# Two-layer vision block on one core: one group's last mixed channels loaded apart and measured two chunks on, steps without pieces spread in one group, constant products at first

## The chip, the cores and the metric

The kernel runs on one core of a Trainium2 chip. The metric is the device time of one execution in microseconds (us), as the median of several runs. A core has a matrix engine (TensorE, in the profile PE for products and PEld for weight loads), VectorE (DVE), ScalarE (ACT), GpSimd (POOL), and SyncE (SP), which here issues every DMA in the order written. The engines run apart from each other and each takes its own instructions in order.

## The reference

The input `x` is (2, 56, 56, 384) in float32: two images of 3136 tokens with 384 channels. Two layers follow each other.

```
# layer 0
h = neighborhood_attention(layer_norm(x), w_qkv, b_qkv, rpb, w_proj, b_proj, heads=12, k=7)
x = x + h
x = x + gelu(layer_norm(x) @ w1 + b1) @ w2 + b2          # 384 -> 1536 -> 384
# layer 1
p = layernorm(x) @ w_in + b_in                            # 384 -> 768
local = depthwise 3x3 convolution of p
mixed = 0.25 * (four running means of local: left, right, up, down) + local
x = x + layernorm(mixed) @ w_out + b_out                  # 768 -> 384
x = x + gelu(layernorm(x) @ w1 + b1) @ w2 + b2
```

In the attention, each token attends to the 7 x 7 tokens around it (moved inward at the borders), with a bias per head and offset. The running means are first-order filters (decay 0.6, gain 0.4) along rows and columns, in both directions.

## The kernel before

**Attention.** The tokens are cut into 14 groups `n` of 448 (8 rows of one image), and each group into 4 windows of 8 x 14 tokens. One window and one of three sets of four heads (`hg`) make a step `s`, so that a group has 12 steps, `k = s % 12`. In step `s` TensorE makes the scores of the step (L515, tile `sc`, two PSUM banks), where two steps with two chunks of keys each share one go; VectorE adds the bias (L530, `pts`), ScalarE takes the exponential, VectorE adds the chunks up (L546, `sum`), and TensorE multiplies the numerators of step `s - 2` with the values (L556, `o`) and adds them up (L563, `sums`). After a window's last set, VectorE turns the sums (L482), GpSimd copies them (L484, `totals`), VectorE inverts them (L488) and watches their size (L492, `good`), GpSimd widens them (L494, `wide`), VectorE turns and multiplies (L498, L500).

Beside the step stands at most one *piece* for later groups, taken from the list `ahead`: a query or key block (L386, six passes of 448 columns) or a tile of values (L424, six passes of 384). At k = 0 the list is filled with 9 or 10 pieces; `spare` names the steps without one, which are (3, 4, 5) where there are 9, and else (4, 6). Up to group 10 a projection of an earlier group (L582) can stand beside the step too. Group 11 has 9 pieces and no projections.

`load_residual(t)` loads a tile of the input for the sum after the projection and sets a count of steps (4 in the first use), after which `add_bias` lets GpSimd add a row to it (L576). The first three tiles are loaded ahead of the step loop, all with the same count.

**Before the step loop.** The first group is normalized, turned by TensorE (L357) and put through the key, value and query products. PSUM tiles come from `any_bank`, four banks in turn. `ident` (128 x 128 unit matrix) and `ones_hd` (128 x 32, all ones) are constants made on chip.

**Layer 0's MLP and layer 1** work on groups of up to 512 tokens. In the last part, `dgroups` are the groups of layer 1's MLP: four tiles of 128 tokens each, the last two groups smaller. `half_way` is the first of them which reaches into the second image; here it is group 6, with 64 tokens of image 0 and 448 of image 1. The convolution and the running means run as jobs of `beside`, an object that puts VectorE work between the products by estimated cost: first `Band` jobs (rows), then per image six `Columns` jobs, one for each 128 of the 768 channels. The job `(1, 5)` is the last one. A `Columns` job ends with two stores of its half images to `mix_d` (L1259). `beside.until(name)` puts out all steps up to the end of a job at once.

`load_mix(g)` loads a group's mixed values, all six channel blocks, to the tile `mx` (L1274). For `half_way` it does so in pieces of 128 tokens, after `beside.until((1, 5))`; it is called behind the last output tile of group 4. While group 5's hidden layer runs, 12 chunks `m` of 6 passes (L1080), `measure_beside` makes the statistics of group 6: `measure` turns one tile of 128 tokens by TensorE (L1288, `xi`) and VectorE takes mean and variance (L214, L215). For `g <= half_way` this is done behind chunks m = 3, 5, 7, 9, and `close`, which makes the inverse deviation (L219 on VectorE, L222 on GpSimd), behind m = 10. Groups after `half_way` are measured on VectorE alone. Behind m = 11 `project_out` multiplies `mx` with `w_out`.

Of the kernel before, what the change touches and what calls it, by code (L numbers as in the profile page):

```python
# [41 lines left out]
NH, KS, HD = 12, 7, 32  # L42
P = 128
NC = C // P
INNER, NI = 2 * C, 2 * C // P
HID, NHID = 4 * C, 4 * C // P
# [127 lines left out]
def block_kernel(ctx: ExitStack, tc: tile.TileContext, ins: dict, out: bass.AP):  # L174
    nc = tc.nc
# [11 lines left out]
    mix_d = [dram.tile([NI, P, H * W], F32, name=f"mix_d{b}") for b in range(B)]  # L187

    ident = const.tile([P, P], F32, name="ident")
# [101 lines left out]
    ones_hd = lp.tile([P, HD], F32, name="ones_hd")  # L291
# [87 lines left out]
    def any_bank():  # L379

        return ps_s.tile([P, GT], F32, name="ps", tag="any")
# [186 lines left out]
    def load_residual(t, pool=lp, bufs=3, steps=4):  # L568

        xrs[t] = pool.tile([P, C], F32, name="xr", bufs=bufs)  # L570
        nc.sync.dma_start(out=xrs[t], in_=xf[t * P : (t + 1) * P, :])
        loaded[t] = steps
# [33 lines left out]
    def load_group(src, group, tag):  # L606
        t0, n = group
        t = xp.tile([P, NT, C], F32, name=tag)
        nc.sync.dma_start(
            out=t[:, :n, :], in_=src[t0 : t0 + n * P, :].rearrange("(k p) c -> p k c", p=P)  # L610
        )
        return t
# [29 lines left out]
            nc.sync.dma_start(out=dst, in_=src)  # L642


    tps = [any_bank() for c in range(NC)]
    halves = [Norm(sm) for h in range(2)]
    for h, norm in enumerate(halves):
# [39 lines left out]
        channels_of(2, c, any_bank)()  # L687
    load_bias(0, 3)
    for t in range(3):
        load_residual(t)  # L690
    shift_by_values(ep, ps_t, wproj, shift)
    sctx.close()

# [13 lines left out]
    for s in range(NU + 4):  # L707
        n, k, hg, i = s // UG, s % UG, s % NC, s // NC
        if s == NU:

            kctx.close()
            xp = ctx.enter_context(tc.tile_pool(name="x", bufs=2, side="right", reuse_waits="tile"))
            tail_pool = actx.enter_context(tc.tile_pool(name="a_tail", bufs=1))
            xs = {g: load_group(x1f, groups[g], "xa") for g in range(2)}
            for t in range(T2 // P - 4, T2 // P):
                load_residual(t, tail_pool, 4, 2)
        store_all()
        while load:
            load_residual(load.pop(0))
        if k == 0 and n < ng:  # L720
            vals = []
            if n + 1 < ng:
                ahead += [lambda n=n, m=m: query_or_key(n + 1, m, one_bank) for m in range(NC)]
                vals += tiles_of(n + 1)[2:]
            if n + 2 < ng:
                vals += tiles_of(n + 2)[:2]
            ahead += [lambda t=t: value(t, one_bank) for t in vals]
            if n + 2 < ng:
                ahead += [
                    lambda n=n, m=m: query_or_key(n + 2, m, one_bank) for m in range(NC, 2 * NC)  # L730
                ]

            spare = (3, 4, 5) if len(ahead) == 9 else (4, 6)

        if k == 2 and n + 4 < ng:
            load_x(n + 4)
        if k == 1 and n < ng:
            load_bias(n, NWC - 1)
        if n + 1 < ng and k in (4, 10):
            load_bias(n + 1, 0 if k == 4 else 1)  # L740
        if s == NU - UG - 4:
            ectx.close()
            wm = ctx.enter_context(tc.tile_pool(name="w_mlp", bufs=1, side="right"))
            w1, w2, w_parts = weights(0)
        if s < NU and hg == 2 and s + 1 < NU:
            ws[i + 1] = Window(i + 1)
        if s >= NU - UG - 4 and hg == 2 and w_parts:
            w_parts.pop(0)()

        if s <= NU:  # L750
            for take in taking:
                take()
            taking = []
        if s == NU + 1:
            sctx.close()
            ps_s = sctx.enter_context(tc.tile_pool(name="a_pss", bufs=4, space=PSUM))
        if s < NU:

            if s not in units:
                units[s] = Unit(ws[i], hg)  # L760
                units[s].scores()
                behind = Unit(ws[(s + 1) // NC], (s + 1) % NC) if s + 1 < NU else None
                if behind is not None and (units[s].m + behind.m) * TT <= BANK:
                    behind.scores(units[s].m)
                    units[s + 1] = behind
        new, before, last = units.get(s), units.get(s - 1), units.pop(s - 2, None)
        done = last.w if last is not None and last.hg == NC - 1 else None
        if last is not None:
            last.values()
        behind = ws.get(i - 1 - (hg == 0))  # L770
        if behind is not None and hg == 2:
            behind.invert()
        if behind is not None and hg == 0:
            behind.divide()
            if behind.j == NWC - 1:
                to_project += tiles_of(behind.n)
            ws.pop(behind.i)
        if n + 3 < ng and k < NT:
            measure_x(n + 3, k)
        for half in range(2):  # L780
            if new is not None:
                new.biased(half)
                new.numerators(half)
            if half == 0 and done is not None:
                done.take()
        if before is not None:
            before.gathered()
        if done is not None:
            done.gather()
        if n < END:  # L790
            if ahead and k not in spare:
                taking.append(ahead.pop(0)())
            if to_project and n < END - 1:
                taking.append(project(to_project.pop(0), turning_bank))
        elif ahead:
            if k != 3:
                taking.append(ahead.pop(0)())
        elif s - END * UG in THEN:
            taking.append(project(to_project.pop(0), one_bank))
        elif s > NU and s < NU + 4 and to_project:  # L800
            taking.append(project(to_project.pop(0), any_bank))
        for t in list(loaded):
            loaded[t] -= 1
            if loaded[t] < 0:
                add_bias(t)
        if n + 3 < ng:
            if k in (4, 5):
                for q in range(2 * k - 8, 2 * k - 6):
                    normalize_x(n + 3, q)
            if k in (8, 9, 11):  # L810
                taking.append(channels_of(n + 3, (8, 9, 11).index(k), turning_bank))
# [159 lines left out]
    def passes(xs, xn, w1, w2, between=lambda ps: None):  # L971
# [12 lines left out]
        beside = Beside()  # L984

        def images(t, n):


            for b in range(B):
                lo, hi = max(t, b * T1), min(t + n, (b + 1) * T1)  # L990
                if lo < hi:
                    yield b, lo - b * T1, lo - t, hi - lo
# [273 lines left out]
        def load_mix(g):  # L1266
            t0, n = dgroups[g]
            mx = io.tile([P, NI, MT], F32, name="mx")

            step = P if g == half_way else n * P  # L1270
            for t in range(0, n * P, step):
                for b, at, here, size in images(t0 + t, step):
                    here += t
                    nc.sync.dma_start(  # L1274
                        out=mx[:, :, here : here + size],
                        in_=mix_d[b][:, :, at : at + size].rearrange("m p t -> p m t"),
                    )
            x = load_group(x2_d, dgroups[g], "xa")
            if g >= half_way:
                add_row(x, dgroups[g][1], "b_out")  # L1280
            return mx, x, Norm(sm)

        def measure(mx, norm, k):
            parts = []
            for h in range(2):
                ps = ps_t.tile([P, NC, P], F32, name="xi", tag="pt")
                for c in range(NC):
                    nc.tensor.transpose(  # L1288
                        ps[:, c, :], mx[:, h * NC + c, k * P : (k + 1) * P], ident
                    )  # L1290
                parts.append(ps.rearrange("p c q -> p (c q)"))
            norm.add(k, parts)
# [12 lines left out]
        def measure_beside(m, g, ahead):  # L1305


            n = dgroups[g][1]
            if g > half_way:
                if m % 2 == 0 and m // 2 < n:  # L1310
                    measure_by_vector(ahead[0], ahead[2], m // 2)
            elif m % 2 == 1 and 0 < m // 2 <= n:
                measure(ahead[0], ahead[2], m // 2 - 1)
            if m == 10:
                ahead[2].close(n)

        def project_out(g, mx, x, inner):
# [174 lines left out]
        for g, (t0, n) in enumerate(dgroups):  # L1492
# [37 lines left out]
                    add_row(x3, dgroups[g + 1][1], "b2_1")  # L1530
                beside.go(ROW_D)
            if g + 2 == half_way:
                beside.until((1, NI - 1))
                ahead = load_mix(g + 2)
        pctx.close()

# [90 lines left out]
```

## Time and profile before

| | us |
|---|---|
| median of 3 runs (lowest, highest) | 2680.19 (2678.64, 2681.08) |
| the profiled execution's own time | 2680.04 |
| its span, first to last instruction | 2678.2 |
| TensorE products of the hidden layers (L1080), busy | 771.1 |
| VectorE busy, all | 1963.2 |
| TensorE clock granted, mean | 0.996 |

The span is what the trace covers; the difference of 1.84 us to the execution's own time lies around it. In 40 slices of about 67 us the page gives the busy tenths of the products and the granted clock:

```profile
PE   8999999999899999999999999999999899999999
...
PEclk9999999999999999999999999999999999999999
```

A 9 means 90% or more, so that only the first slice, the eleventh and the thirty-second show idle time here, and a few microseconds at a lower clock do not show at all. In lists of instructions below, a line has the start, the duration, the engine, the line of the kernel, the operation, what it writes and reads, the tile sizes and types and how many were merged, and in brackets the idle time just before it with what ended it.

### The profile page before, as it was taken

The page shows a single profiled execution, that of the slowest core. Times are in us where ns is not written, and L with a number is a line of the kernel's source. Part 1 is how long each engine was busy: PE and PEld are TensorE (multiplying, and loading weights), DVE is VectorE, ACT ScalarE, POOL GpSimd, SP SyncE. Part 2 cuts the span into 40 slices and gives each one's busy share as a digit, 9 for nine tenths or more (in the row PEclk, how much of TensorE's full clock was granted, in tenths as well). Part 3 has the DMA queues.
Part 4 walks back from the last instruction along what each step waited for, and adds up shares of the span by engine and source line. Part 5 has one row for each costly group of instructions (what it writes and reads, how often), then busy time and mean ns, then how long its engine had stood idle before and what let it go on. Part 6 is the DMA issues. An engine that isn't in the chain of part 4 may idle for free. (4 is left out here: it accounts for less than half of the span.)

```text
span 2678.2 us, 37275 instructions
## 1 busy us (share of the span) xinstructions
PE 2640.3 (99%) x14963; PEld 1473.9 (55%) x14963; DVE 1963.2 (73%) x3539; ACT 898.7 (34%) x1447; POOL 249.7 (9%) x264
## 2 busy tenths in 40 slices
PE   8999999999899999999999999999999899999999
PEld 4666666656655455555555555555555455555556
DVE  3778877876365698688989889888988627677652
ACT  4555555554322332223344422311143211111111
POOL 1111111111211100000010000000010011101100
PEclk9999999999999999999999999999999999999999
DMA  6323454224411132233346544533346401111000
GB/s 216 134 89 102 154 170 146 80 77 158 156 37 38 65 107 88 89 128 105 123 156 230 184 149 150 178 120 114 118 182 228 152 19 37 45 44 39 30 12 17
DMA packets 134249, 298.99 MB, mean 112 GB/s; under 512 B 11463, under 2 KB 89905, under 8 KB 131761
## 3 DMA queue, kind: packets, MB, share of 16 engines
q1 hardware_dynamic: 134064, 296.50, 32.3%
q8 instruction: 119, 1.95, 0.3%
q14 instruction: 66, 0.53, 0.1%
HBM read 180.86 MB, written 115.61 MB: 111 GB/s over the span
## 5 line engine op out<-in xcount | busy, mean ns | idle before, releaser
L1080 PE MATMUL mm<-hT,w 128*128 128x512 f32 (+2 forms) x1872 | 771.1, 569 | 0.4 <-ACT hT L254 0.2
L1080 PEld LDWEIGHTS mm<-hT,w 128*128 128x128 f32 x1872 | 352.7, 190 | 383.5 <-issue 352.1
L1089 ACT ACTIVATE hid<-mm,chan 128x512 f32<-128x512 f32 (+2 forms) x312 | 206.1, 661 | 683.3 <-PE mm L1080 683.2
L1096 PE MATMUL y_end<-w,hid 128*128 128x384 f32 x1200 | 395.2, 486 | 0.0
L1174 DVE SCALAR_TENSOR_TENSOR loc<-pt,taps,loc 128x990 f32<-128x990 f32 (+9 forms) x336 | 377.1, 1122 | 10.0 <-ACT loc L1156 1.7
L1096 PE MATMUL y<-w,hid 128*128 128x384 f32 x1152 | 379.4, 486 | 0.0
L1096 PEld LDWEIGHTS y_end<-w,hid 128*128 128x128 f32 x1200 | 227.5, 190 | 157.2
L1096 PEld LDWEIGHTS y<-w,hid 128*128 128x128 f32 x1152 | 218.2, 190 | 150.5 <-issue 1.0
L530 DVE TENSOR_TENSOR pts<-sc,bias 119x448 f32<-119x448 f32 (+3 forms) x336 | 220.9, 699 | 78.2 <-PE sc L515 75.2
L536 ACT ACTIVATE pts<-pts 119x448 f32<-119x448 f32 (+3 forms) x336 | 206.8, 642 | 191.3 <-DVE pts L530 187.9
L222 POOL TENSOR_TENSOR rs<-rs,mhalf 128x4 f32<-128x4 f32 (+4 forms) x67 | 87.1, 1300 | 1727.0 <-DVE rs L219 1691.6
L386 PE MATMUL ps<-hT,wqkv 128*128 128x448 f32 x504 | 212.0, 559 | 2.0 <-ACT qT L396 0.7
L1064 DVE STREAM_TRANSPOSE hT<-xn 32x96 f32<-32x96 f32 x672 | 181.1, 269 | 31.4 <-PE mm L1080 11.8
L1080 PE MATMUL mm<-hT,w_in 128*128 128x512 f32 (+2 forms) x468 | 191.9, 568 | 0.6 <-ACT hT L254 0.6
L240 ACT ACTIVATE xn<-xc,sh,rs 128x384 f32<-128x384 f32 x98 | 64.7, 698 | 268.6 <-DVE sh L233 268.5
L1080 PEld LDWEIGHTS mm<-hT,w_in 128*128 128x128 f32 x468 | 88.5, 190 | 102.1 <-issue 90.6
L386 PEld LDWEIGHTS ps<-hT,wqkv 128*128 128x128 f32 x504 | 90.2, 191 | 82.8 <-issue 73.1
L515 PEld LDWEIGHTS sc<-qT,kT 32*100 32x100 f32 (+3 forms) x3168 | 91.6, 170 | 67.1 <-issue 17.9
L1299 DVE STREAM_TRANSPOSE turned<-mx 32x192 f32<-32x192 f32 x336 | 123.3, 367 | 4.2
L515 PE MATMUL sc<-qT,kT 32*100 32x112 f32 (+3 forms) x3168 | 114.7, 272 | 6.5 <-DVE pts L530 5.8
L556 PE MATMUL o<-pts,vt 100*32 100x112 f32 (+3 forms) x3168 | 112.7, 266 | 3.8 <-DMA vt<-v_d 2.7
L582 PE MATMUL ps<-wproj,og 128*128 128x384 f32 x294 | 107.1, 503 | 3.6 <-DVE xr L590 3.6
(104 smaller groups left out, 2644.9 us busy)
## 6 DMA issues: line engine op xcount, KB each, us to landing
bias<-in_bias_t SPq DMA_DIRECT2D x16, 1344.0 KB
loc<-loc_d SPq DMA_DIRECT2D x24, 784.0 KB
mixed<-mix_d SPq DMA_DIRECT2D x24, 784.0 KB
mix_d<-mixed SPq DMA_DIRECT2D x24, 784.0 KB
xa<-x_d SPq DMA_DIRECT2D x22, 768.0 KB
p_d<-mx SPq DMA_DIRECT2D x10, 1536.0 KB
mx<-mix_d SPq DMA_DIRECT2D x10, 1536.0 KB
pt<-p_d SPq DMA_DIRECT2D x18, 560.0 KB
```

The source lines that it names most:

```text
L386: nc.tensor.matmul(ps, lhsT=wqkv[:, c, m * P : (m + 1) * P], rhs=hT[:, c, half_of(n)], start=c == 0, stop=c == NC - 1,)
L515: nc.tensor.matmul(sc[i // 2][: w.keys, i % 2, (first + c) * TT : (first + c + 1) * TT], lhsT=kT[d, hg, w.keys_at + r * w.kc : w.keys_at + ...
L530: nc.vector.tensor_tensor(self.of(half), sc[half][:n, :, at].rearrange("p h (c q) -> p h c q", q=TT), self.w.bias[:n, 4 * self.hg + h : 4 ...
L536: nc.scalar.activation(self.of(half), self.of(half), AF.Exp)
L556: nc.tensor.matmul(o[i * HD : (i + 1) * HD, hg, :], lhsT=w.vt[:n, c, h * HD : (h + 1) * HD], rhs=self.pts[:n, i, c, :], start=c == 0, stop ...
L582: nc.tensor.matmul(ps, lhsT=ogs[t // 7][:, c, at : at + P], rhs=wproj[:, c, :], start=c == 0, stop=c == NC - 1,)
L1064: nc.vector.transpose(hT[j : j + HD, :, k * P + i : k * P + i + HD], xn[i : i + HD, k, :].rearrange("p (c q) -> p c q", c=NC)[:, :, j : j ...
L1080: nc.tensor.matmul(ps[:, : n * P], lhsT=w[:, c, m * P : (m + 1) * P], rhs=hT[:, c, : n * P], start=c == 0, stop=c == NC - 1,)
L1089: nc.scalar.activation(t[:, : n * P], ps[:, : n * P], AF.Gelu, bias=col(b1, m))
L1096: nc.tensor.matmul(ps, lhsT=t[:, k * P : (k + 1) * P], rhs=w[:, m, :], start=m == 0, stop=m == len(lhs) - 1,)
L1174: nc.vector.scalar_tensor_tensor(to, pt[:, lo + dy - self.top : hi + dy - self.top, xt : xt + n], self.tap(dy, dx), to, ALU.mult, ALU.add,)
L1299: nc.vector.transpose(t[j : j + HD].rearrange("p (m c) -> p m c", m=NI)[:, :, i : i + HD], mx[i : i + HD, :, k * P + j : k * P + j + HD],)
```

## The change

There are four edits. Before the first group's work, twelve products of `ones_hd` and `ident` are written to a bank that nothing reads. The first three residual tiles get a count of 8 steps in place of 4. In group 11 (`END - 1`) the steps without a piece are k = 3, 6, 9. For `half_way`, the mixed values are loaded in two parts: channel blocks 0 to 4 after the job (1, 4), block 5 after the job (1, 5), each for all tokens of the group in one DMA per image; its tiles are measured behind m = 5, 7, 9, 11 and the statistics closed behind m = 11.

```
+    warm = any_bank()
+    for _ in range(12):
+        nc.tensor.matmul(warm[:HD, :P], lhsT=ones_hd, rhs=ident, start=True, stop=True)
     tps = [any_bank() for c in range(NC)]
...
     for t in range(3):
-        load_residual(t)
+        load_residual(t, steps=8)
...
             spare = (3, 4, 5) if len(ahead) == 9 else (4, 6)
+            if n == END - 1:
+                spare = (3, 6, 9)
...
             mx = io.tile([P, NI, MT], F32, name="mx")
-            step = P if g == half_way else n * P
-            for t in range(0, n * P, step):
-                for b, at, here, size in images(t0 + t, step):
-                    here += t
+            def load_channels(lo, hi):
+                for b, at, here, size in images(t0, n * P):
                     nc.sync.dma_start(
-                        out=mx[:, :, here : here + size],
-                        in_=mix_d[b][:, :, at : at + size].rearrange("m p t -> p m t"),
+                        out=mx[:, lo:hi, here : here + size],
+                        in_=mix_d[b][lo:hi, :, at : at + size].rearrange("m p t -> p m t"),
                     )
+            if g == half_way:
+                beside.until((1, NI - 2))
+                load_channels(0, NI - 1)
+                beside.until((1, NI - 1))
+                load_channels(NI - 1, NI)
+            else:
+                load_channels(0, NI)
...
                     measure_by_vector(ahead[0], ahead[2], m // 2)
-            elif m % 2 == 1 and 0 < m // 2 <= n:
-                measure(ahead[0], ahead[2], m // 2 - 1)
-            if m == 10:
+            else:
+                late = 2 if g == half_way else 0
+                k = (m - late) // 2 - 1
+                if m % 2 == 1 and 0 <= k < n:
+                    measure(ahead[0], ahead[2], k)
+            if m == (NHID - 1 if g == half_way else 10):
                 ahead[2].close(n)
...
             if g + 2 == half_way:
-                beside.until((1, NI - 1))
                 ahead = load_mix(g + 2)
```

## What was predicted

> **What bounds the kernel now.** I read the busy line of the page first, then the waits of TensorE, then a table of 50 us stretches to see where its idle time lies, and last the timeline at each such place.
>
> ```profile
> PE 2640.3 (99%) x14963; PEld 1473.9 (55%) x14963; DVE 1963.2 (73%) x3539; ACT 898.7 (34%) x1447; POOL 249.7 (9%) x264
> ```
>
> TensorE is the bound: only 38 of 2678.2 us are not matmul. But a matmul at half clock also counts as busy, so the clock must be read beside it. In the waits of TensorE (awaited; us in total, times, longest):
>
> ```profile
> PE xi L1288 <- DMA mx<-mix_d: 7.7, 1, 7.7
> PE ps L357 <- DVE xg L226: 7.0, 1, 7.0
> PE sc L515 <- DVE pts L530: 5.8, 10, 1.3
> ```
>
> One wait in the middle, one at the start, and small ones on VectorE. In the stretches (PE, PEld, DVE, ACT, POOL busy; then granted clock, DMA share, GB/s), these two matter most; from 750 to 2100 us PE is full in nearly every one (0 to 50 has 42.33, for its start):
>
> ```profile
> 550.00:600.00 50.00, 47.45 (x711) 29.55 (x709) 37.35 (x72) 25.15 (x46) 5.62 (x11) 0.93 0.18 62
> ...
> 2100.00:2150.00 50.00, 42.34 (x128) 22.32 (x127) 25.67 (x32) 7.84 (x12) 3.43 (x1) 0.93 0.61 197
> ```
>
> The two 0.93 are stretches with about 7 us at a clock of 0.5.
>
> [...]the clock is 0.50 from 583.9 to 590.7 and from 2130.1 to 2137.0[...]. The window 580.47 to 583.88 with 1.85 us of matmuls lost it, 577.06 to 580.47 with 2.90 did not; 583.88 to 587.29, full but two thirds small attention products, did not win it back. [...]7.04 to 10.45 was 2.97 us busy, mostly transposes, and stayed slow. [...]here the first `xg` load was issued at 0.74 and used at 3.18.
>
> **Part A: the mixed channels of group 6 (`half_way`).** The timeline:
>
> ```profile
> 2123.26 1.10 SPq L1259 DMA_DIRECT2D mix_d<-mixed  x2
> 2124.41 7.00 SPq L1274 DMA_DIRECT2D mx<-mix_d  x5
> ...
> 2132.52 1.51 PE L1288 MATMUL xi<-ident,mx 128*128 128x128 f32 x6 [7.67 <-DMA mx<-mix_d]
> ...
> 2133.83 6.86 PE L1080 MATMUL mm<-hT,w 128*128 128x512 f32 x12
> ```
>
> The five loads of all six channels stand behind the last column's stores. TensorE stops 7.67 us at chunk m = 3 and then works at half clock: the first pair of chunks with its transposes takes 8.01 us (`xi` at 2132.52, again at 2140.53), the next 5.81 (to 2146.34). Loss 7.67 + 2.20 = 9.87 us.
>
> After the change, channels 0 to 4 (two DMAs) stand on SP after the last `out` store of group 4 and ahead of the column's stores: by the built order nothing else moves past them. They can issue at about 2116, need two issues (1.1 to 1.9 us each here) and 1.3 MB at some 400 GB/s, and are in by 2121; SP is free again before 2123.26, when the stores can first go. The last channel's load for image 0 needs no store; that for image 1 needs the first store only: SP's one wait here lets it go near 2126.6. A sixth of the bytes (0.23 MB, 0.6 us) behind the rest of the second store[...]: landed at 2129.5 to 2131. The first transpose that needs it is the last of six at m = 5. Chunks take 2.58 us from 2114.40, so six are out at 2129.9, and 0.7 later it is reached. Left over: 0 to 0.6 us, I take 0.3[...]. What is late next: the statistics of the fourth tile, at m = 11, close straight before the projection. Its scale is there after about 2.3 us (bn_stats 0.5, aggregate 0.2, L219 0.15, POOL 1.0, hand-overs), and the first projection's 12 products of 0.33 us take 4.0: hidden, 1.7 us to spare. The `xa` load and the next `mx` move about 4 us earlier and wait for nothing. Gain A: 9.87 - 0.3 = **9.6** (8.3 to 9.9).
>
> **Part B: group 11's steps without a piece.** Now at k = 3, 4, 5, with no projections beside them:
>
> ```profile
> 582.71 0.44 PE L515 MATMUL sc<-qT,kT 32*100 32x112 f32 x4 [1.12 <-DVE pts L530]
> 583.47 1.10 PE L515 MATMUL sc<-qT,kT 32*100 32x112 f32 x20 [0.33 <-DVE pts L530]
> ...
> 586.15 4.21 PE L424 MATMUL ps<-wqkv,hT 128*128 128x384 f32 x6
> ```
>
> A bare step is 1.68 us of TensorE, but VectorE needs 1.62 (bias) + 1.23 (sums) + 0.71 (a third of a window's 2.13) = 3.56 us. Three in a row make TensorE wait, [...]and the value at 586.15 takes 4.21 where the next one, at 592.13, takes 2.20. From 574.61 to 590.29 there are 15.68 us for 3 x 1.68 + 1.68 + 2.13 = 8.85 us of work: 6.8 lost. At k = 3, 6, 9: a bare step still delays the next scores until the bias has freed their bank, 0.95 us at k = 3 by this timeline (T + 0.87 + 1.62 before the next can end), some 0.75 at k = 6, and near 0.2 at k = 9, whose scores are made in a pair with k = 10. Between them stand two steps with pieces of 3.9 us, in which VectorE catches up. 1.9 us stay; a window around one bare step has 2.7 us of products, over the 2.40 that kept the clock at 669.2 to 672.6. Values go out earlier, keys 13 still before they are read; SP's `v_d` stores move ahead of two `vt` loads that have two steps of slack. Gain B: **4.9** (3.0 to 5.5).
>
> **Part C: `steps=8`.**
>
> ```profile
> 63.56 2.90 POOL L576 TENSOR_TENSOR xr<-xr,shift 128x384 f32<-128x384 f32 x3
> ...
> 63.78 1.75 DVE L492 SCALAR_TENSOR_TENSOR good<-totals,good 128x11 f32<-128x11 f32 x2
> ...
> 70.01 0.40 PE L563 MATMUL sums<-sum,ones_hd 120*32 120x112 f32 x8 [1.17 <-DVE sum L546]
> ...
> 72.44 0.31 DVE L492 SCALAR_TENSOR_TENSOR good<-totals,good 128x11 f32<-128x11 f32 x2
> ```
>
> The three adds hold up `good` by 1.44 us and the copy `wide` to 66.40. Moved behind the second window's `wide` (72.58), they run to about 76. Without them the chain bias, sum, reciprocal ends 1.26 us earlier and the wait at 70.01 shrinks. There VectorE may be stretched by the same 1.5 us, but the next scores come at 80.25 and VectorE idles 3.46 us before them: hidden. If that slack were gone, 1.5 comes back. Gain C: **1.2** (0 to 1.5).
>
> **Part D: the twelve products at first.** Two passes each, 24 of 128 columns: at half clock [...]5.1 us from 1.65, ends near 6.8; with the transposes' 11% over that rate, 7.35. The transposes begin at 7.02 now, so it is 0 to 0.5 late. The possible gain: the clock is low until 13.86 (weight loads 0.75 us apart, then 0.375). Five products x 0.375 + 0.4 on the transposes = 2.3 us if the clock is there by 7.0 and stays. But these products fill 32 columns of the array, like the attention products that did not win the clock back, and then transposes follow. I take **0** (-0.5 to 2.4).
>
> **The sum.** 9.6 + 4.9 + 1.2 + 0 = 15.7. The profiled execution took 2680.04 us (span 2678.2 and 1.84 around it), 0.15 under the median of 2680.19: 2680.04 - 15.7 = **2664.3**. Low clock windows near 655 and 680 (one each) may come and go[...]: 1.7 us each way.
>
> **Rivals.**
> 1. *The wait in the middle only moves.* For it: the last channel still hangs on the same store, and one `xa` and a 1.5 MB `mx` load follow at once. Against: they are issued later and it is a sixth of the bytes. If it lands only at 2138 with them, the stop is about 7.5 us and the clock goes again: A gives 0 to 2, total 2673.
> 2. *The first products do win the clock.* [...]Against: their columns. 2664.3 - 2.3 = 2662.0.
> 3. *Slower: the clock stays low through group 11.* [...]now three bare steps can lose it. Losing it at each for two windows costs 10.2 us in place of 3.2 and leaves about 5 in all, the edge of no change. If it is low from k = 3 to k = 11, 29 us of TensorE work doubles: 2680.0 - 10.8 - 6.8 + 29 = 2691. It is slower by 0.2% from 23 us of work at low clock on.[...]
>
> **How the numbers follow.** The forecast 0.68 (its own range 2660 to 2669), rival 1 0.15, rival 2 0.12, rival 3 0.05. A measurement tells 0.2% (5.4 us) from no change. Faster: 0.68 + 0.12 + 0.12 of rival 1 = 0.92; same 0.03; slower 0.05. The range 2658 to 2671 takes in rival 2 and the near half of rival 1.
>
> **What would show it.** A: the wait of `xi` on `mx` under 1 us and no clock of 0.5 near 2110 to 2140; wrong if `xi` waits over 3. B: the value products of group 11 all 2.2 us per six, waits of `sc` on `pts` in three places; wrong if the clock dips there. C: `good` 0.31 in the second window, no 1.17 before `sums`. D: weight loads still 0.75 us apart from 10 to 13; wrong if 0.375 at once. The forecast falls if A or B does.

## The result, and the profile after

| | before | after |
|---|---|---|
| median, us (lowest, highest; runs) | 2680.64 (2678.64, 2681.68; 4) | 2663.61 (2661.53, 2667.66; 4) |
| span of the profiled execution, us | 2678.2 | 2660.6 |

The ratio is 0.9939 with a 95% interval of 0.9922 to 0.9956: 17.0 us faster. The forecast was 2664.3. On a later occasion nine runs of before lay between 2678.76 and 2684.67, and five more runs of after had a median of 2664.79.

The busy line and the waits of TensorE of after (waited for; us in total, times, longest):

```profile
PE 2637.1 (99%) x14987; PEld 1473.8 (55%) x14987; DVE 1960.8 (74%) x3539; ACT 899.1 (34%) x1447; POOL 250.3 (9%) x264
```

```profile
PE sc L515 <- DVE pts L530: 4.5, 7, 1.3
PE ps L582 <- DVE xr L590: 2.6, 2, 2.1
PE o L556 <- DMA vt<-v_d: 1.8, 1, 1.8
PE ps L648 <- DVE ones_hd L292: 1.7, 1, 1.7
PE ps L386 <- ACT vs L431: 1.5, 1, 1.5
```

The wait of `xi` on the mixed channels, 7.7 us before, is gone from the list. So is the 7.0 us wait at the start, but there 24 passes of the new products (L648) now fill the time. A wait on a `vs` buffer is new against before, though no_warm and only_mix, which don't have the new products, show it too. The two stretches with a clock of 0.93 before (length, then busy time of PE, PEld, DVE, ACT, POOL, then clock, DMA share, GB/s):

```profile
550.00:600.00 50.00, 47.41 (x747) 29.56 (x745) 39.59 (x76) 27.54 (x51) 5.62 (x11) 1.00 0.23 73
...
2100.00:2150.00 50.00, 50.00 (x149) 25.83 (x148) 22.77 (x35) 9.53 (x14) 4.45 (x2) 1.00 0.42 148
```

Both run at full clock (1.00). From 550 to 600 the busy time of PE is the same as before (47.45), but now it holds 747 passes where 711 stood: of the time that the earlier profile showed as busy, 583.87 to 590.70 was spent at a clock of 0.50. The low clock of before in the other stretch, 2130.10 to 2136.93, is gone as well. Between their start and their end, these two traces have a clock of 0.50 for 3.41 or 6.83 us at a time; where the recorded texts count windows, one is 3.41 us.

**Where the 17.6 us between the spans lie.** The table cuts each profile at the same instructions of TensorE: *start* to the first scores (L515); *residual* from there to the third value product (L424) after it; *group 11* from the last turn of `xg` (L357) to the last query product (L386); *attention's end* from there to the first L251; *half_way* from the turn (L251) for group 5 to the one for group 6, the last two turns of this line, between which the mixed channels come; *rest* from there to the end of the span. The two stretches left out, 493.2 and 1397.6 us, are equal within 0.04 in every row but one: in early_measure the second is 1.7 us longer, and a clock of 0.50 from 702.9 to 709.7 reaches into it.

| profile | start | residual | group 11 | attention's end | half_way | rest | span |
|---|---|---|---|---|---|---|---|
| before | 46.31 | 24.02 | 55.26 | 88.93 | 91.31 | 481.55 | 2678.2 |
| after | 46.41 | 22.77 | 51.37 | 87.14 | 81.28 | 480.79 | 2660.6 |
| only_mix | 47.99 | 24.04 | 55.16 | 88.55 | 81.47 | 480.76 | 2668.8 |
| only_spare | 47.04 | 24.03 | 51.36 | 89.24 | 91.46 | 481.56 | 2675.5 |
| no_warm | 46.61 | 22.77 | 51.35 | 89.55 | 81.28 | 480.83 | 2663.2 |
| early_measure | 45.97 | 22.77 | 51.36 | 92.07 | 88.00 | 480.79 | 2673.5 |
| one_load | 46.86 | 22.77 | 51.37 | 89.63 | 83.63 | 481.59 | 2666.7 |
| spare_even | 46.52 | 22.77 | 48.46 | 90.51 | 81.28 | 480.74 | 2661.1 |
| vs3 | 44.93 | 22.76 | 51.36 | 87.05 | 81.29 | 480.81 | 2659.0 |
| best | 44.76 | 22.77 | 48.46 | 86.76 | 81.28 | 480.76 | 2655.6 |

The parts of the change stand alone in their columns: half_way 10.03 us, group 11 3.89, residual 1.25, start -0.10. No run has `steps=8` alone, but residual is 24.0 in the three profiles without it and 22.8 in the seven with it. The start moves by more than 0.10 by itself; what moves it is shown with vs3 below. The rest gives 0.76, which the prediction didn't have. Attention's end gives 1.79 here, but this column runs from 86.8 to 92.1 without any edit in it, so this isn't counted as the change's.

**Half_way, after** (the timeline):

```profile
2108.82 1.03 SPq L1278 DMA_DIRECT2D mx<-mix_d  x2
...
2116.14 1.11 SPq L1265 DMA_DIRECT2D mix_d<-mixed  x2
...
2117.30 2.85 SPq L1278 DMA_DIRECT2D mx<-mix_d  x2
...
2123.03 0.82 PE L1301 MATMUL xi<-ident,mx 128*128 128x128 f32 x6
...
2128.84 0.82 PE L1301 MATMUL xi<-ident,mx 128*128 128x128 f32 x6
```

Two of the loads now precede the stores at 2116.14, and the six transposes of `xi` at 2123.03 wait for nothing: no bracket stands behind the line. From 2123.03 to 2128.84 are 5.81 us at a clock of 1.00, the pace of before once its clock was back (2140.53 to 2146.34). At the other end, where the statistics close late:

```profile
2141.11 4.04 PE L1102 MATMUL y<-w_out,mx 128*128 128x384 f32 x12
...
2142.59 1.02 POOL L222 TENSOR_TENSOR rs<-rs,mhalf 128x4 f32<-128x4 f32 x1 [13.48 <-DVE rs L219]
...
2145.25 0.62 DVE L1339 SCALAR_TENSOR_TENSOR xc<-y,rs,xa 128x384 f32<-128x384 f32 x1 [2.80 <-PE y L1102]
```

The scale `rs` is ready at 2143.61, 1.54 us before the first projection ends; VectorE waits for `y`, not for `rs`.

**Group 11, after.** TensorE around the three steps without a piece (*bare steps*):

```profile
575.25 0.44 PE L515 MATMUL sc<-qT,kT 32*100 32x112 f32 x4 [0.23 <-DVE pts L530]
576.01 0.82 PE L515 MATMUL sc<-qT,kT 32*100 32x112 f32 x20 [0.33 <-DVE pts L530]
...
577.48 2.20 PE L424 MATMUL ps<-wqkv,hT 128*128 128x384 f32 x6
...
586.05 0.82 PE L515 MATMUL sc<-qT,kT 32*100 32x112 f32 x20 [0.33 <-DVE pts L530]
...
591.51 2.52 PE L386 MATMUL ps<-hT,wqkv 128*128 128x448 f32 x6
594.61 1.10 PE L515 MATMUL sc<-qT,kT 32*119 32x112 f32 x32 [0.58 <-ACT kT L411]
...
598.15 0.40 PE L563 MATMUL sums<-sum,ones_hd 100*32 100x112 f32 x8 [0.96 <-DVE sum L548]
598.48 2.52 PE L386 MATMUL ps<-hT,wqkv 128*128 128x448 f32 x6
```

The values take 2.20 us, no longer 4.21. Behind two of the bare steps the next scores (at 575 and 586) wait for banks as foreseen. The third, whose scores stand at 594, waits elsewhere: for a key, and then, at 598, for the sum of k = 8.

**Residual, after**:

```profile
63.88 0.31 DVE L492 SCALAR_TENSOR_TENSOR good<-totals,good 128x11 f32<-128x11 f32 x2
...
68.85 0.40 PE L563 MATMUL sums<-sum,ones_hd 120*32 120x112 f32 x8 [0.68 <-DVE sum L546]
...
71.91 1.95 POOL L576 TENSOR_TENSOR xr<-xr,shift 128x384 f32<-128x384 f32 x2
```

`good` takes 0.31 in place of 1.75, the wait before `sums` is 0.68 in place of 1.17, and the additions stand behind the second window's `wide`.

**Start, after** (TensorE; then VectorE's first work on group 1; then ScalarE):

```profile
1.73 5.30 PE L648 MATMUL ps<-ident,ones_hd 128*32 128x128 f32 x24 [1.73 <-DVE ones_hd L292]
...
9.64 7.03 PE L386 MATMUL ps<-hT,wqkv 128*128 128x448 f32 x18 [0.62 <-ACT hT L362]
16.51 5.97 PE L424 MATMUL ps<-wqkv,hT 128*128 128x384 f32 x18
...
25.71 1.77 PE L386 MATMUL ps<-hT,wqkv 128*128 128x448 f32 x4 [1.49 <-ACT vs L431]
```

```profile
16.04 0.56 DVE L214 BATCH_NORM_STATS2 st<-xg 112x6 f32<-112x384 f32 x1 [7.50 <-DMA xg<-in_x]
```

```profile
20.32 2.50 ACT L240 ACTIVATE xg<-xg,sh,rs 112x384 f32<-112x384 f32 x4 [2.70 <-DVE sh L233]
22.72 0.83 ACT L431 COPY vs<-ps 128x384 f32<-128x384 f32 x2
25.18 0.48 ACT L431 COPY vs<-ps 128x384 f32<-128x384 f32 x1 [1.62 <-DMA v_d<-vs]
```

The 18 passes at 9.64 take 7.03 us where they took 8.94 before, with a clock of 1.00 from 7.73 on where it came at 13.84, and the values start at 16.51 where before they started at 18.74. But the next query product stands at 25.71; before, it stood at 25.70. In between, ScalarE first normalizes group 1 (L240), in the order written, and that waits for the load of group 1, on which VectorE starts at 16.04. So the copies of the values start at 22.72, although the first tile of values is done near 18.5 (six passes from 16.51). Then the third copy to `vs` waited 1.62 us for the store that frees one of its two buffers.

### The profile page after: what moved, and what is told of

Same layout as the page of the kernel before. It is cut to its first block, busy times and chain, and to the rows that moved or that the text cites. A ratio compares the mean times of both kernels' runs of the same rounds, so it can differ in the third digit from the quotient of the medians.

```text
span 2660.6 us, 37324 instructions
## 1 busy us (share of the span) xinstructions
PE 2637.1 (99%) x14987; PEld 1473.8 (55%) x14987; DVE 1960.8 (74%) x3539; ACT 899.1 (34%) x1447; POOL 250.3 (9%) x264
## 5 line engine op out<-in xcount | busy, mean ns | idle before, releaser
L386 PE MATMUL ps<-hT,wqkv 128*128 128x448 f32 x504 | 210.2, 555 | 3.6 <-ACT vs L431 1.5
L240 ACT ACTIVATE xn<-xc,sh,rs 128x384 f32<-128x384 f32 x98 | 64.7, 698 | 269.0 <-DVE sh L233 268.9
L386 PEld LDWEIGHTS ps<-hT,wqkv 128*128 128x128 f32 x504 | 89.4, 189 | 83.3 <-issue 71.6
L515 PEld LDWEIGHTS sc<-qT,kT 32*100 32x100 f32 (+3 forms) x3168 | 91.5, 170 | 65.8 <-issue 15.6
L515 PE MATMUL sc<-qT,kT 32*100 32x112 f32 (+3 forms) x3168 | 114.2, 272 | 5.7 <-DVE pts L530 4.5
L556 PE MATMUL o<-pts,vt 100*32 100x112 f32 (+3 forms) x3168 | 112.3, 266 | 2.9 <-DMA vt<-v_d 1.8
```

Source lines behind the costliest of these rows:

```text
L386: nc.tensor.matmul(ps, lhsT=wqkv[:, c, m * P : (m + 1) * P], rhs=hT[:, c, half_of(n)], start=c == 0, stop=c == NC - 1,)
L515: nc.tensor.matmul(sc[i // 2][: w.keys, i % 2, (first + c) * TT : (first + c + 1) * TT], lhsT=kT[d, hg, w.keys_at + r * w.kc : w.keys_at + ...
L556: nc.tensor.matmul(o[i * HD : (i + 1) * HD, hg, :], lhsT=w.vt[:n, c, h * HD : (h + 1) * HD], rhs=self.pts[:n, i, c, :], start=c == 0, stop ...
```

## The experiments

Theory: three of the parts each give their time in their own stretch, and the new products nothing. Rivals: only one half of the mixed-channel edit works; moving the bare steps only moves the wait; the products do speed up the start. Every kernel below computes the whole reference. A ratio is to before, with its interval.

**only_mix and only_spare**: the kernel before with only the edits to `load_mix` and `measure_beside`, and with only

```
+            if n == END - 1:
+                spare = (3, 6, 9)
```

> The kernel before with the edit of the mixed channels alone (two loads, measured behind m = 5, 7, 9, 11). Theory: the stop of 7.67 us and the two windows of half clock after it go, nothing else; 10.0 us faster, about 2670.5, with no wait of xi on mx and a clock of 1.00 around the middle. Rival (the whole gain is more than the sum of parts[...]): clearly less than 8.

> The kernel before with steps 3, 6, 9 of group 11 bare in place of 3, 4, 5. Theory: 3.9 us between the start of step 3 and the key product that follows step 12 are saved, as in the traces of before and after (36.6 to 32.7), with no low clock there; about 2676.7. Rival ([...]spread steps can lose it as well): a clock of 0.5 between 574 and 612, and a gain under 1.

only_mix: 2671.15 us (2670.6 to 2671.53, 5 runs), ratio 0.9963 (0.9949 to 0.9977). only_spare: 2678.12 (2674.3 to 2680.66, 20 runs), ratio 0.9990 (0.9983 to 0.9997). In the table each moves its own column: half_way 91.31 to 81.47, group 11 55.26 to 51.36. Yet the median of only_spare is only 2.6 us under that of before, and the range covers 6 us. Its start is 0.73 us longer than in before, because the load of group 1 came 0.64 later (16.11 against 15.47), and its attention's end 0.3 us. The time of a stretch and the time of the execution are two things to look up here.

**early_measure and one_load**: the two halves of the mixed-channel edit, in the changed kernel. early_measure keeps the apart load and measures as before, behind m = 3, 5, 7, 9. one_load keeps the late measuring and loads all six channels after the last job, as before.

```
# early_measure
-                late = 2 if g == half_way else 0
+            elif m % 2 == 1 and 0 < m // 2 <= n:
+                measure(ahead[0], ahead[2], m // 2 - 1)
# one_load
-                beside.until((1, NI - 2))
-                load_channels(0, NI - 1)
...
+            step = P if g == half_way else n * P
```

> The changed kernel with the load in two parts kept, but group 6 measured behind m = 3, 5, 7, 9 as before. Theory (both halves of the edit are needed: the last channel lands some 14 us after the first chunk starts, and m = 3 ends after 10.3): xi waits about 3.5 us for mx at m = 3, and the stretch from the last turn of group 5 to that of group 6 (turns on TensorE, L251) is 84.5 to 86.5 us in place of 81.28. Rival (the load in two parts does it alone): 81.3.

> The changed kernel with all six channels loaded behind the last column as before, in pieces of 128 tokens, and measured behind m = 5, 7, 9, 11. Theory: the first piece lands 18.1 us after the first chunk starts, as before, and m = 5 ends after 15.5: xi waits 2.7 us, the clock stays or is lost for one window; the same stretch is 84 to 85.7 us. Rival (the later measurement does it alone): 81.3.

early_measure took 2675.29 us, one_load 2668.57 (one run each); half_way is 88.00, longer than expected because the clock went as well (0.50 for 3.41 us), and 83.63, somewhat shorter than expected. Their waits at the mixed channels, early_measure first:

```profile
2124.07 0.71 PE L1301 MATMUL xi<-ident,mx 128*128 128x128 f32 x5
...
2129.61 0.39 PE L1301 MATMUL xi<-ident,mx 128*128 128x128 f32 x1 [4.83 <-DMA mx<-mix_d]
2129.80 6.96 PE L1086 MATMUL mm<-hT,w 128*128 128x512 f32 x12
```

Five transposes pass and only the sixth waits: five channels are there, the last isn't. It waits 4.83 us, and the next products take 6.96 where 5.32 is the pace: the clock was 0.50 from 2129.68 to 2133.09. In one_load:

```profile
2128.31 0.85 PE L1294 MATMUL xi<-ident,mx 128*128 128x128 f32 x6 [2.16 <-DMA mx<-mix_d]
...
2128.99 5.32 PE L1086 MATMUL mm<-hT,w 128*128 128x512 f32 x12
```

Here all six wait, 2.16 us, and the clock stays at 1.00. Half_way is 6.72 us longer than in after without the late measuring and 2.35 longer without the apart load. So both halves are needed, and the late measuring is the larger one.

**spare_even**: the changed kernel with other bare steps in group 11.

```
-                spare = (3, 6, 9)
+                spare = (0, 2, 10)
```

> The changed kernel with steps 0, 2, 10 of group 11 bare in place of 3, 6, 9; these three have no scores of their own, since two steps are scored together there. Theory (a bare step costs where the next scores wait for the bias of this one, and at k = 9 for a sum too, 2.9 us in all in the changed kernel): from the last turn before group 11 to the last query product 49.0 us in place of 51.37, time 2.3 us less, 2661.3. Rival (VectorE's 3.56 us for each step of three chunks hold TensorE, so that six such steps with pieces in a row are no better): 51 or more.

2663.59 us (2663.01 to 2665.09, 4 runs), ratio 0.9933 (0.9916 to 0.9949): no different from after. Group 11 did become 2.91 us shorter (48.46), so that most of what the bare steps left over in after was a matter of which steps they are. In this profile the attention's end, in turn, was 3.37 us longer. From the waits of TensorE:

```profile
PE o L556 <- DMA vt<-v_d: 8.0, 6, 2.9
PE sc L515 <- DVE pts L530: 2.4, 3, 1.3
```

VectorE's wait is down from 4.5 to 2.4, and the wait for loads of values is up from 1.8 to 8.0, in one profile. That the other bare steps cause this isn't shown: after_again has 5.9 us of this wait without them, and best, with them, has 3.8 us and an attention's end of 86.76.

**no_warm, and after once more**: the changed kernel without the twelve products; the first no_warm was not run together with after; after_again and no_warm_again were.

> The changed kernel without the twelve products at first. Theory (they win the clock, but the lead of 2.2 us that TensorE has at the first value products is eaten behind them, where the third copy of values waits for a store): the first scores of the step loop start at 46.3 as before, and the time is that of the changed kernel within 0.5 us, 2663.6. Rival (the lead is real and only a late load of group 1 hid it in the profiled execution): 2 us slower than the changed kernel, 2665.7.

> The changed kernel once more, on the same chip and in the same rounds as no_warm_again, to settle the twelve products' worth. Before group 11 they move first scores by 0.2 us (46.41 against 46.61 in the first pair). If that is all, the two medians differ by less than 1 us. If they also change what follows, this one is 2 to 3 us faster, as in the first pair (2663.6 against 2666.0). Its profile also tells whether the early clock (first value product at 16.5 us) comes again.

> The changed kernel without the twelve first products, once more. If they are worth 0.2 us, its median is within 1 us of after_again; if they are worth what the first pair showed, it is 2 to 3 us slower. First value product at 18.4 us or later, first scores at 46.0 to 48.0 us.

First no_warm had 2666.01 us (2664.76 to 2668.76, 4 runs) against 2663.61 of after, which looked like 2.4 us for the products. In the second pair after_again had 2664.79 (2662.66 to 2666.14, 5 runs) and no_warm_again 2664.58 (2662.82 to 2667.29, 5 runs): no difference. With the nine runs of each put together, the medians are 2664.79 and 2664.95. The 2.4 us were the spread of four runs: between the first two profiles, attention's end made 2.41 of the 2.6 us of span, and first scores 0.20, as much as the load of group 1 came later (16.25 against 16.04). In after_again the clock came early again (values at 16.50), its first scores stand at 46.30, and its attention's end is 91.00 us, 3.9 longer than in after, with the same instructions.

**vs3 and vs3_no_warm**: a third buffer for `vs`, with and without the products.

```
-            vs = ep.tile([P, C], F32, name="vs", bufs=2)
+            vs = ep.tile([P, C], F32, name="vs", bufs=3)
```

> The changed kernel with three buffers for the value tiles (vs) in place of two. Theory: the third copy of values no longer waits for the first store, the wait of 1.49 us before the query products at 25.71 goes, and the first scores start near 45.0; about 1.4 us faster than the changed kernel, 2662.2. Rival (the store is not what holds it; the copies stand behind the normalization on ScalarE, which waits for the load of group 1): the query products start at 25.2 or later, under 0.5 us gained.

> The changed kernel with three value buffers and without the twelve products at first. Theory (third buffer and clock are worth something only together): first scores at 46.2 to 46.8, no wait for the value copy, time within 0.7 us of the changed kernel without the products, 2666. Rival (the buffer is the whole gain of vs3): first scores near 45.

vs3: 2660.37 us (2659.24 to 2661.75, 4 runs), ratio 0.9922 (0.9906 to 0.9939). vs3_no_warm: 2666.21 (2664.69 to 2667.8, 4 runs), ratio 0.9941 (0.9924 to 0.9958). In vs3 all copies run in one go, and the query product follows 1.40 us earlier than in after:

```profile
22.98 1.20 ACT L431 COPY vs<-ps 128x384 f32<-128x384 f32 x3
```

```profile
16.79 5.97 PE L424 MATMUL ps<-wqkv,hT 128*128 128x384 f32 x18
...
24.31 3.20 PE L386 MATMUL ps<-hT,wqkv 128*128 128x448 f32 x8
```

First scores are at 44.93, 1.48 us earlier than in after. The buffer's own share shows when one counts from VectorE's first L214 on group 1, which follows the load; it stands anywhere from 14.85 to 17.62 us in the fourteen profiles. In vs3:

```profile
16.29 0.56 DVE L214 BATCH_NORM_STATS2 st<-xg 112x6 f32<-112x384 f32 x1 [7.48 <-DMA xg<-in_x]
```

From there to the first scores are 28.64 us, and the same in best. With two buffers they are 30.36 to 30.43 in eight profiles, whether the values start at 16.50 (after_again) or at 19.23 (only_mix). So the third buffer is worth 1.7 us, and the earlier values are worth nothing in these eight: the load sets the first scores. Only where the copies wait for TensorE's values instead is it longer, by an estimated 0.5 to 1.3 us: 30.84 in before, 30.93 in only_spare, 31.67 in rows32.

Without the products, in vs3_no_warm, the values start at 19.73, the copies don't wait for buffers (their waits are for TensorE), and first scores are at 47.30, later than expected and 31.56 us behind L214. In these profiles the third buffer pays only together with an early clock, and the early clock, in the main, only with the third buffer.

**rows32**: the products with 32 of their 128 rows.

```
-        nc.tensor.matmul(warm[:HD, :P], lhsT=ones_hd, rhs=ident, start=True, stop=True)
+        nc.tensor.matmul(warm[:HD, :P], lhsT=ones_hd[:HD, :], rhs=ident[:HD, :], start=True, stop=True)
```

> The changed kernel with its twelve first products cut to 32 rows, 32 by 32 into 32 by 128. If it is TensorE's being occupied that counts for the clock, whatever part of the array works, weight loads of the key pass take 0.375 us from about 9.6 us on and the first value product starts at 16.4 to 16.8 us. If the share of the array counts, the clock comes with the key passes themselves and the first value product starts at 18.2 us or later.[...]

2662.72 us (one run). The first value product starts at 18.95, so the clock came late. With all 128 rows the values started at 16.5 to 16.8 in five profiles (after, after_again, vs3, one_load, best), but at 18.21 in spare_even and 18.40 in early_measure. The products of spare_even, then of rows32:

```profile
1.73 5.03 PE L648 MATMUL ps<-ident,ones_hd 128*32 128x128 f32 x24 [1.73 <-DVE ones_hd L292]
```

```profile
1.73 5.29 PE L648 MATMUL ps<-ident,ones_hd 32*32 32x128 f32 x24 [1.73 <-DVE ones_hd L292]
```

In spare_even the last passes are 0.11 us apart in place of 0.21. The clock in the trace agrees: spare_even and early_measure do win it, at 6.35 and 6.59, and lose it again for 3.41 us (9.76 to 13.17 and 10.00 to 13.41). So all seven profiles with 128 rows have the full clock by 7.73, the six without products from 13.01 to 15.49, and rows32 from 14.25. In rows32 these products fill 3.02 us between 4.01 and 7.43, and the clock stays low until 14.25; in after, those with 128 rows fill 2.71 us between 4.32 and 7.73, where it rises. That speaks for the share of the array, in one profile; more isn't shown. First scores at 46.52, as early as in after (46.41), say nothing on this: VectorE started on group 1 at 14.85 here, 1.2 us earlier than in after.

**best**: vs3 and spare_even together.

> The changed kernel with both of the pieces that did best: three buffers for vs, and group 11's spare lists of two with a remainder. If the two savings add up, first scores stand at about 45.0 us (46.4 in the changed kernel), the stretch of group 11 is 48.5 us (51.4), the stretch of the last attention is below 71 us, and the median lies between 2657.0 and 2659.5 us. If what is won in group 11 is only waited for again at the value loads of the last attention, as in spare_even, that stretch is 72 to 75 us with several microseconds of waiting for vt's loads, and the median is that of vs3, 2660.4 us within 1 us.

2660.71 us (2657.43 to 2661.71, 5 runs), before 2682.01 on the same occasion; ratio 0.9919 (0.9905 to 0.9932). The profiled execution, 2657.43, holds both gains: start 44.76, group 11 48.46, attention's end 86.76. The median is that of vs3. Five runs can't say whether the change of the bare steps is worth 0 or 2 us on top.

## Why the prediction was right

**Part A, 9.6 forecast: right.** The column half_way gives 10.03, and only_mix alone 9.84. The two losses named, 7.67 of waiting and 2.20 of low clock, went entirely; the leftover wait of 0.3 was not there, since the last block was in before 2123.03. The landing time foreseen, 2129.5 to 2131, was the author's estimate (its rate of some 400 GB/s is near the 386 that before has from 2136.93 to 2140.30), and so was that a wait of 0.3 us leaves the clock alone; the shortest one measured at this place, 2.16 us in one_load, did. (Times of after stand 6.82 us before those of before here: the first issue foreseen at 2116 came at 2115.64 on that scale.) The slack for the late `close`, forecast at 1.7 us, measured 1.54. That the channels are loaded apart *and* measured late was needed: see early_measure and one_load. Rival 1, that the wait only moves, is in part what happens with one half of the edit.

**Part B, 4.9 forecast, 3.89 measured.** The mechanism held in the main: no low clock (1.00 from 550 to 600), values at 2.20, waits at all three bare steps, but on `pts` only at two of them. That a single bare step keeps the clock was an estimate from three stretches of 3.41 us in before: behind 2.90 and 2.40 us of products the clock was 1.00, behind 1.85 it was 0.50. How much is enough isn't shown beyond these. The mis-sized term is "near 0.2 at k = 9". Taken from the end of one piece to the start of the next, less the products between them (a product's length is the distance to the next start where nothing is awaited), the bare steps lose 4.01 - 2.95 = 1.06 us at k = 3 (forecast 0.95), 4.30 - 3.33 = 0.97 at k = 6 (0.75), and 4.51 - 2.86 = 1.65 at k = 9 (0.2). The pairing of k = 9 with k = 10 was taken as a relief, since no bank is awaited. But it leaves k = 10 without scores, so that only the product of k = 8 with the values (L556) stands between the sums of k = 7 and those of k = 8, and VectorE hasn't added these up: 0.96 us. The key made at k = 8, which the scores read, adds 0.58. So 3.7 us stayed in place of 1.9. That this cost only 1.0 of the gain is because the loss of before was larger, too: spare_even is 6.80 us shorter than before and still has the wait of 0.58, so at least 7.4 us were lost there, and the forecast had 6.8.

**Part C, 1.2 forecast, 1.25 measured: right**, by the path that it named. Beside the additions `good` took 1.75 us, away from them 0.31; why they hold it up isn't shown. VectorE is stretched where foreseen, a sum to 0.87 us from 0.61 and a product to 0.73 from 0.51, and still waits 2.98 us for the next scores.

**Part D, 0 forecast: right in size by luck, wrong in its reason.** The step that failed is "these products fill 32 columns of the array, like the attention products that did not win the clock back". The twelve products take 5.30 us, close to the estimate of 5.1 (24 passes of 128 columns at the 0.75 us that 448 columns took in before). And they did win the clock: weight loads are 0.375 us apart from 10.88 on, where the forecast said that they would still be 0.75 apart, and the value products start 2.23 us earlier, close to the 2.3 that rival 2 had. What was missing is the question of who takes over the lead. ScalarE copies the values only behind the normalization of group 1, and that hangs on the load of group 1, so no copy starts before 22.72. The third copy then needs a buffer, which the first store to `v_d` has to free: 1.62 us more. From VectorE's first work on that load to the first scores are 30.4 us, however early the values are; with a third buffer 28.6 (vs3, best). The start was also foreseen right in that the transposes begin 0 to 0.5 late: 7.05 in place of 7.02.

**What the sum left out.** The rest of the run gained 0.76 us. It is at the very end: from the issue of the last store to the end of the span. Before, then after:

```profile
2674.67 0.34 SPq L1557 DMA_DIRECT2D out<-rows  x1
```

```profile
2657.83 0.34 SPq L1572 DMA_DIRECT2D out<-rows  x1
```

These are 3.53 us to the end of the span before and 2.77 after. The shorter one goes with the mixed channels loaded in two parts: with spans not rounded it is 2.75 to 2.77 us in the eleven profiles that have them, and 3.54 to 3.57 in the three that don't (before, only_spare, one_load). Why the last store takes less then is open.

So 9.6 + 4.9 + 1.2 became 10.03 + 3.89 + 1.25 = 15.17 in the places named, 0.5 under the forecast; with 0.76 at the end and 1.1 from places that vary, 17.0 in the medians. That the median came within 0.7 us of the forecast is in part luck: the 1.0 us that B lacked was more than made up by A's extra 0.4 and by 1.9 us that no part of the forecast had named.

**What stays open**: why the attention's end varies by 5 us between executions of nearly the same instructions. Two things go with it, low clock and waits for `vt` loads: after has 6.83 us of low clock there and 1.8 us of waits for `vt`, after_again 10.24 and 5.9. Over the fourteen profiles the low clock there makes 3.4 to 10.2 us and these waits 1.8 to 8.0. The forecast's 1.7 us each way for the low clock, an estimate of the author's, was too small for both together. Which comes first, the late load or the clock, was not tried.

## What to carry to other kernels

An input that comes late is best met from both sides: load early what is ready, and ask for the rest as late as the next step's slack allows; each half alone left 2.4 or 6.7 of 10 us here. When an edit makes a stage start earlier, follow the lead forward to the first buffer or load that doesn't move with it; at the start of this kernel 2.2 us were lost behind a load and a buffer, and a third buffer let 1.7 us through. And where a stretch varies by more than the effect, judge an edit by its own stretch in the profile and by many runs: four runs of each showed 2.4 us for twelve products that nine runs of each do not.

## What the hardware showed unexpectedly

- Twelve float32 products of 128 x 32 with 128 x 128, 24 passes in 4.06 to 5.30 us, come with an early full clock on TensorE though their weights have 32 columns where the key products' have 128: it came at 4.37 to 7.73 us in all seven profiles that have them, at 13.01 to 15.49 in the six without. In two of the seven it was lost again for 3.41 us; why is open. With a quarter of the rows as well, it came at 14.25 in the one profile.
- The clock changes at other times from run to run of one kernel (13.01 us in no_warm, 13.66 in no_warm_again).
- Over a wait of 2.16 us at the mixed channels the clock stayed at 1.00, one of 4.83 us was followed by a clock of 0.50 for 3.41 us (2129.68 to 2133.09), and the 7.67 of before by one for 6.83 (2130.10 to 2136.93).
